# A graph layer on one core: edge attributes and window sums on ScalarE's DMA queue, and other requests moved in time

## The chip, the core and the metric

The kernel runs on one core of a Trainium2 chip. A core has five instruction queues. TensorE (PE) multiplies matrices, VectorE (DVE) and ScalarE (ACT) work on vectors, GpSimd (POOL) here issues gathers, and SyncE (SP) here issues plain DMA transfers. ScalarE can issue plain transfers as well. Each queue works in order and waits on semaphores that the others raise. The metric is the time of the whole program on the device in microseconds (us), the median of several runs.

## The reference

x has 12,500 nodes of 128 features, and there are 400,000 edges, sorted by target. Cut to what matters, in float32:

```
h       = relu(layernorm(x))
msg_src = h @ w_src + b_src;   msg_dst = h @ w_dst
rad     = silu(silu(edge_attr @ w1 + b1) @ w2 + b2) @ w3 + b3      # 400000 x 128 from 32 attributes
m       = (msg_src[src] + msg_dst[dst]) * edge_weight * rad
a, v    = m @ w_a + b_a, m @ w_v + b_v                             # 8 heads of 16 each
score   = sum over a head of smooth_leaky_relu(a) * alpha_dot
att     = softmax of score over the edges of one target
out     = x + segment_sum(v * att, dst) @ w_proj + b_proj
```

## The kernel before

**Node stage.** The nodes go in 25 groups of up to four 128-row blocks (`quads`). x is loaded whole by eight SP transfers (L157, L158). For each group i, `norm` (L231, ACT) makes h, `turn` transposes it (L240 PE, L243 DVE), and `products` multiplies by both weights (L255 PE), copies the result into a tile `ms` (L261 ACT, L259 DVE for some) and asks SP for the two stores to the tables t_src and t_dst (L266). `ms` has four buffers, so a copy waits until the stores from four groups earlier have landed. After group 1 SP issues `load_targets` (L178 to L185, five transfers) and then `load_weights` (L195 to L205). After group 12 stands `fits` (a test of the sorted targets on DVE, a small product on PE, and the load of the sections' first and last targets into `eb`), and after group 20 `cuts`, which reads `eb` and some of the weights.

**Edge stage.** `windows()` goes through 400 pairs; a pair is 1000 edges, two sections of 500. `step(k)` writes one iteration out in the order in which each engine meets its instructions; nothing reorders them later. Its steps are shifted against each other: loads are asked for some pairs ahead, the gathers four and five ahead, the first MLP layers three to one ahead, and the second half, with `c = k - 12`, is twelve pairs behind. In the order of the code, step k has on SP the store of the 128 x 136 sums of pair c-1 into `win` (`store_win`, L926), the store of half of them into `agg` at a row that is read from a table first (`store(c-1, 0)`, L929 and L930), the edge weights of pair k+3 (`load_w`, L717), the rows of targets of pair k+3 (`load_md`: two `value_load` of a row number, L721, and two transfers of 64 x 128, L723), in odd steps the targets of two pairs (`load_d`, L711), the attributes of pair k+6 (`load_e`, L706, 125 x 8 x 32 elements, which lie in runs of 128 bytes), every eighth step a row of marks (`load_sm`, L852), and the second half of the sums (`store(c-1, 1)`). From step 40 on, every eight steps, a block of x is loaded (`load_x`, L937, at the sixth of the eight steps) and two steps later has a bias added on DVE and is stored (`add_x`, L944, L945).

Then comes the arithmetic: `split_md` 0 (L729 ACT: rows of targets of pair k+1 to bf16), `weights` (L888 ACT), `mlp3` (L794 PE, L798 DVE), `sources(k, 1)` (L807 PE: four transposes of gathered rows), `gather(k+4, 1)` (L743 POOL: four gathers into the buffer that `sources(k, 1)` has just released), `message` (L815 PE, L820 DVE into `mT`), `values(c, 0)` (L907 PE, L909 DVE), `split_md` 1 (L732 DVE), `alphas(k, 0)` (L824 PE, L826 ACT into `sl`, L828 DVE), `split_md` 2 (L734 ACT), `mlp1(k+2)` (L762 PE, L765 ACT), `values(c, 1)`, `one_hot(c)` (L894, L897 DVE), `sources(k+1, 0)`, `gather(k+5, 0)`, `alphas(k, 1)`, `mlp2(k+1)` (L777 PE, L780 ACT), `one_hot_T` (L787 DVE), `split_md` 3 (L736 DVE), `sums(c)` (L918 PE, L922 ACT into `ob`, three buffers), `e_T(k+3)` (L753 PE, L755 ACT: the transposed attributes), and in odd steps `scores` (L835 PE, L838 ACT, and the store L840 by SP). `mlp1`, `mlp2` and `mlp3` use the same PSUM tile, so the product of each waits until ACT or DVE has read the one before.

**Lanes.** All plain transfers share eight semaphores in turn. A transfer waits for the one before it on its semaphore, besides the tiles that it needs. A transfer on ACT's queue waits in the same way, and what follows it on that queue waits with it.

**Last stage.** After pair 399 fourteen more steps empty the second half, while the sums of sections that share a target are put together from `win` (`rows_load`, L1074) and scattered into `agg`; then `fin` reads `agg`, multiplies by w_proj and stores the output.

Of the kernel before, what the change touches and what calls it, by code (L numbers as in the profile page):

```python
# [21 lines left out]
F32 = mybir.dt.float32  # L22
# [8 lines left out]
P = 128  # L31
C = 128
# [24 lines left out]
def gnn_kernel(ctx: ExitStack, tc: tile.TileContext, a: dict, out: bass.AP):  # L57
    nc = tc.nc
# [19 lines left out]
    win = dram.tile([NS * W, ROW], F32, name="win")  # L78
# [18 lines left out]
    Q = len(quads)  # L97
# [51 lines left out]
    with tc.tile_pool(name="node", bufs=2) as np_, tc.tile_pool(name="node1", bufs=1) as n1, \  # L149
# [26 lines left out]
        def load_targets():  # L176

            nc.sync.dma_start(out=cur[:, 1:CC + 1], in_=dst.rearrange("(p c) -> p c", p=P))  # L178
            at = dst[CC - 1:CC]
            with nc.allow_non_contiguous_dma(reason="single targets"):  # L180
                nc.sync.dma_start(out=cur[1:P, 0:1], in_=bass.AP(at.tensor, at.offset, [[CC, P - 1], [1, 1]]))
                for f in range(2):
                    nc.sync.dma_start(out=base[:, f, :], in_=dst_h[f:f + 1, :, 0])
                at = dst[0:1]
                nc.sync.dma_start(out=ends, in_=bass.AP(  # L185
                    at.tensor, at.offset, [[8 * SEC, 100], [SEC, 8], [SEC - 1, 2]]))

        def load_weights():
            for name, t in wt.items():
                ap = a[name]  # L190
                if name == "b_src":
                    ap = ap.rearrange("o c -> c o")
                elif name == "b_proj":
                    ap = ap.to_broadcast([P, C])
                nc.sync.dma_start(out=t, in_=ap)  # L195
            for f in range(2):
                for q in range(2):
                    o = (2 * q + f) * RAD
                    nc.sync.dma_start(out=w1b[o:o + RAD, f * FC:(f + 1) * FC], in_=a["fc_w1"])
                s = slice(f * FC, (f + 1) * FC)  # L200
                for q in range(2):
                    nc.sync.dma_start(out=w2b[s, q * FC:(q + 1) * FC], in_=a["fc_w2"])
                nc.sync.dma_start(out=w3b[s, :], in_=a["fc_w3"])
                nc.sync.dma_start(out=b12[s, 0:1], in_=a["fc_b1"])
                nc.sync.dma_start(out=b12[s, 1:2], in_=a["fc_b2"])  # L205
# [40 lines left out]
        def products(i):  # L246
            t0, t1 = quads[i]
            hT = hTs.pop(i)
            ms = np_.tile([P, 2, 4, C], F32, name="ms", bufs=4)
            for v0 in range(t0, t1, 2):  # L250
                vs = range(v0, min(v0 + 2, t1))
                pm = nps.tile([P, 2, 2, C], F32, name="pm", bufs=4)
                for t in vs:
                    n = rows(t)
                    nc.tensor.matmul(pm[:n, t - v0], hT[:, t - t0, :n], w_nodes, start=True, stop=True)  # L255
                for n, u0, u1 in blocks(v0, vs[-1] + 1):
                    o, q = ms[:n, :, u0 - t0:u1 - t0, :].rearrange("p k j c -> p j k c"), pm[:n, u0 - v0:u1 - v0]
                    if v0 % 16 == 2:
                        nc.vector.tensor_copy(o, q)  # L259
                    else:  # L260
                        nc.scalar.copy(o, q)  # L261
            f1 = min(t1, NF)
            for k, table in enumerate((t_src, t_dst)):
                tv = table[0:NF * P, :].rearrange("(p t) c -> p t c", t=NF)
                if t0 < f1:
                    nc.sync.dma_start(out=tv[:, t0:f1, :], in_=ms[:, k, 0:f1 - t0, :])  # L266
                if t1 > NF:
                    nc.sync.dma_start(out=table[NF * P:N, :], in_=ms[:tail, k, NF - t0, :])
# [63 lines left out]
        for i in range(Q):  # L332
            if i % 2 == 0 and 4 * i + G < NB:
                stats(4 * i + G, min(4 * i + 2 * G, NB))
            if i + 2 < Q:
                norm(i + 2)
            if i + 1 < Q:
                turn(i + 1)
            products(i)
            if i == 1:  # L340
                load_targets()
                load_weights()
            if i == 12:
                fits()
            if i == 20:
                cuts()
# [313 lines left out]
    def windows():  # L660
        src_t = src.rearrange("(t p) -> t p", p=T)
        dst_t = dst.rearrange("(t p) -> t p", p=T)
        ea_t = ea.rearrange("(k j p) c -> k p j c", j=8, p=T)
        dst_p = dst.rearrange("(k f e) -> f k e", f=2, e=SEC)
        ew_p = ew.rearrange("(k e) o -> o k e", e=PR)
        with tc.tile_pool(name="wk2", bufs=2) as sp, tc.tile_pool(name="ps", bufs=1, space=PSUM) as pp, \
                tc.manual_schedule(), ExitStack() as held:
            lp = held.enter_context(tc.tile_pool(name="ld", bufs=2))
            prep, e_g, d_g, w_g, md, gath = {}, {}, {}, {}, {}, {}
            eTs, h1s, h2s, ohT, m3, mr, mTs, als, S_all, sms, Ps, Pem, pvx, ohs, accs, xs, Ms, pms = (  # L670
                {} for _ in range(18))
# [31 lines left out]

            def load_e(k):
                e_g[k] = lp.tile([T, 8, RAD], F32, name="e_t", bufs=4)
                nc.sync.dma_start(out=e_g[k], in_=ea_t[k])  # L706

            def load_d(g):
                d_g[g] = lp.tile([P, 2, SEC], I32, name="d_b")
# [7 lines left out]
                nc.sync.dma_start(out=w_g[k], in_=ew_p[:, k, :].to_broadcast([P, PR]))  # L717

            def load_md(k):
                md[k] = lp.tile([P, C], F32, name="md", bufs=4)  # L720
                at = [nc.sync.value_load(base[0:1, f, k:k + 1]) for f in range(2)]  # L721
                for f in range(2):
                    nc.sync.dma_start(out=md[k][f * W:(f + 1) * W, :], in_=t_dst[ds(at[f], W), :])  # L723
# [199 lines left out]
                accs[c] = ob  # L923

            def store_win(c):
                nc.sync.dma_start(out=win[c * P:(c + 1) * P, :], in_=accs[c])  # L926

            def store(c, f):
                at = nc.sync.value_load(base[0:1, f, c:c + 1])  # L929
# [17 lines left out]
            def has(k):  # L947
                return 0 <= k < NP
# [5 lines left out]
            def step(k):  # L954
                c = k - LAG
                if has(c - 1):
                    store_win(c - 1)
                    store(c - 1, 0)

                if k % 16 == 4 and has(k + 12):  # L960
                    prep_load((k + 12) // 16)
                if has(k + 3):
                    load_w(k + 3)
                    load_md(k + 3)
                if k % 2 and has(k + 3):
                    load_d((k + 3) // 2)
                if has(k + 6) and k >= -4:
                    load_e(k + 6)
                if has(k + 4) and (k + 4) % MP == 0:
                    load_sm((k + 4) // MP)  # L970
                if has(c - 1):
                    store(c - 1, 1)
                if 0 <= 2 * k < NZ:
                    for i in range(2 * k, min(2 * k + 2, NZ)):
                        zero(i)
                if k % 16 == 8 and has(k + 8):
                    prep_make((k + 8) // 16)
                i, q = divmod(k - 40, MP)
                if 0 <= i < Q and q == 5:
                    load_x(i)  # L980
                if 0 <= i < Q and q == 7:
                    add_x(i)
                if has(k + 1):
                    split_md(k + 1, 0)
                if has(c):
                    weights(c)
                rad = mlp3(k) if has(k) else None
                if has(k):
                    sources(k, 1)
                if has(k + 4):  # L990
                    gather(k + 4, 1)
                if has(k):
                    message(k, rad)
                if has(c):
                    values(c, 0)
                if has(k + 1):
                    split_md(k + 1, 1)
                if has(k):
                    alphas(k, 0)
                if has(k + 1):  # L1000
                    split_md(k + 1, 2)
                if has(k + 2):
                    mlp1(k + 2)
                if has(c):
                    values(c, 1)
                    one_hot(c)

                if has(k + 1):
                    sources(k + 1, 0)
                if has(k + 5):  # L1010
                    gather(k + 5, 0)
                if has(k):
                    alphas(k, 1)
                if has(k + 1):
                    mlp2(k + 1)
                    one_hot_T(k + 1)
                    split_md(k + 1, 3)
                if has(c):
                    sums(c)
                m, r = divmod(k, MP)  # L1020
                if has(k - MP):
                    if r == 1:
                        softmax_up(m - 1)
                    elif r == 2:
                        softmax_down(m - 1)
                        softmax_exp(m - 1)
                    elif r == 3:
                        softmax_T(m - 1)
                if has(k + 3):
                    e_T(k + 3)  # L1030
                if has(k) and k % 2 == 1:
                    scores(k)
# [300 lines left out]
```

## Time and profile before

| | |
|---|---|
| median of 9 runs | 5890.25 us (5867.07 to 5921.33) |
| profiled execution | 5903.68 us, its span 5901.9 us |
| PE busy | 4619.1 us (78%) |
| POOL busy, 3200 gathers and little else | 3114.7 us (53%) |
| DVE busy | 3096.8 us (52%) |
| ACT busy | 1907.3 us (32%) |
| transfers on SP's queue | 572.15 MB in 796,664 packets |
| mean granted TensorE clock | 0.890 |

A row of a group names line, engine, operation, what is written and read, and how often; then its busy time, the mean of one in ns, and the idle time of the engine just before it with what ended that. "DVE rad <- PE p" in the list of waits means that DVE was idle before `rad` until PE finished `p`. In a timeline the first number is the start in us and the second the duration; what stands in brackets is the engine's idle time before. Issuing a transfer does not count as busy time. The profiled execution took 13.4 us more than the median of the runs, which is within their spread.

### The profile page before, as it was taken

The numbers are of one execution on the slowest core, as the hardware profiler recorded it, in microseconds if no ns is written. First come the engines' busy times: TensorE is split into PE (matmuls) and PEld (weight loads), VectorE is DVE, ScalarE is ACT, GpSimd is POOL, SyncE is SP. The second block draws the span as 40 slices with busy tenths as digits, with TensorE's granted clock in tenths as the row PEclk, the third lists the DMA queues.
The fourth block names the chain that finished last, engine by engine and source line by source line (L and its number), as shares of the span: only waits on it lengthen the run. The fifth ranks groups of instructions, "written<-read, shape, count | busy, mean of one in ns | idle before, by whom it ended". The sixth has DMA issues, their size and how long they took to land.

```text
span 5901.9 us, 88079 instructions
## 1 busy us (share of the span) xinstructions
PE 4619.1 (78%) x29692; PEld 2535.9 (43%) x29692; DVE 3096.8 (52%) x6005; ACT 1907.3 (32%) x4595; POOL 3114.7 (53%) x3223
## 2 busy tenths in 40 slices
PE   5588787787888788777877787888877878878774
PEld 3244444444444444444444444444444444444444
DVE  5355555555555555554555554555555555555556
ACT  4233333333333333333333333333333333333321
POOL 1655555555555555555555555555555555555510
PEclk8789989899898999888898998988898989998887
DMA  5565555555555555555555555555555555555533
GB/s 183 152 150 133 132 136 141 130 132 136 138 136 135 140 132 141 141 127 130 139 129 134 139 133 124 135 134 131 132 129 127 135 129 134 137 134 131 129 85 144
DMA packets 901338, 794.77 MB, mean 135 GB/s; under 512 B 530270, under 2 KB 776974, under 8 KB 900746
## 3 DMA queue, kind: packets, MB, share of 16 engines
q1 hardware_dynamic: 796664, 572.15, 36.1%
q0 software_dynamic: 102816, 210.37, 17.3%
q10 hardware_dynamic: 1394, 6.53, 0.3%
q8 instruction: 234, 3.83, 0.3%
q14 instruction: 230, 1.88, 0.1%
HBM read 648.39 MB, written 140.67 MB: 134 GB/s over the span
## 4 chain that ended last, share of the span: by engine, by line
PE 71%; another core or an unknown queue 8%; DVE 8%; issue 7%; ACT 3%; DMA 2%; SPq 1%; POOL 0%; ACTq 0%; POOLq 0%; DVEq 0%
PE V L907 15%; PE pa L824 13%; PE p L794 8%; PE pm L807 8%; PE misc L918 7%; PE pm L815 5%; PE misc L835 4%; PE p L762 4%; PE p L777 4%; PE m L753 2%; DVE mT L820 2%; DVE rad L798 1%; DVE pvx L909 1%; ACT sl L826 1%
## 5 line engine op out<-in xcount | busy, mean ns | idle before, releaser
L743 POOL DMA_INDIRECT gs<-t_src,idx x3200 | 3100.3, 969 | 2553.1 <-PE pm L807 1158.1
L826 ACT ACTIVATE sl<-pa,c_b_a 128x500 f32<-128x500 f32 x800 | 541.9, 677 | 2403.1 <-PE pa L824 1267.0
L824 PE MATMUL pa<-mT,c_w_a 128*128 128x500 f32 x1600 | 917.8, 658 | 419.8 <-DVE mT L820 297.3
L798 DVE SCALAR_TENSOR_TENSOR rad<-p,c_fc_b,w_b 128x500 f32<-128x500 f32 x800 | 553.2, 733 | 1152.7 <-PE p L794 707.0
L907 PE MATMUL V<-c_w_v,mT 128*125 128x128 f32 x6208 | 980.7, 306 | 182.8 <-DVE pvx L909 161.6
L907 PEld LDWEIGHTS V<-c_w_v,mT 128*125 128x125 f32 x6208 | 823.1, 206 | 502.1 <-issue 273.5
L828 DVE SCALAR_TENSOR_TENSOR al<-pa,sl 128x500 f32<-128x500 f32 x800 | 542.1, 678 | 633.9 <-ACT sl L826 364.3
L909 DVE TENSOR_TENSOR pvx<-V,Pem 125x512 f32<-125x512 f32 x776 | 532.8, 687 | 590.3 <-remote 165.6
L820 DVE SCALAR_TENSOR_TENSOR mT<-pm,c_b_src,rad 128x500 f32<-128x500 f32 x800 | 554.6, 732 | 181.6 <-remote 60.8
L918 PE MATMUL misc<-pvx,oh 125*64 125x136 f32 x6400 | 476.0, 292 | 147.7 <-DVE oh L897 80.3
L807 PE MATMUL pm<-ident,gs 125*128 125x125 f32 x3200 | 560.4, 303 | 1.5 <-DMA gs<-t_src,idx 1.5
L807 PEld LDWEIGHTS pm<-ident,gs 125*128 125x128 f32 x3200 | 404.0, 156 | 351.2 <-issue 348.2
L794 PE MATMUL p<-h,w3b 64*128 64x500 f32 x1600 | 505.5, 712 | 41.7 <-ACT h L780 38.8
L918 PEld LDWEIGHTS misc<-pvx,oh 125*64 125x64 f32 x6400 | 372.1, 141 | 314.8 <-issue 202.6
L824 PEld LDWEIGHTS pa<-mT,c_w_a 128*128 128x128 f32 x1600 | 263.3, 207 | 478.7 <-DVE mT L820 334.0
L835 PE MATMUL misc<-al,w_s 128*32 128x500 f32 x1600 | 255.5, 707 | 258.8 <-ACT ob L922 159.6
L815 PE MATMUL pm<-ohT,m 64*128 64x500 bf16 x2400 | 341.7, 393 | 0.0
L780 ACT ACTIVATE h<-p,b 128x500 f32<-128x500 f32 x400 | 269.8, 674 | 137.4 <-remote 120.7
L922 ACT COPY ob<-misc 128x136 f32<-128x136 f32 x400 | 109.0, 272 | 634.9 <-PE m L753 315.9
L762 PE MATMUL p<-eT,w1b 64*128 64x250 f32 x1600 | 309.9, 468 | 1.0 <-ACT eT L755 0.5
L777 PE MATMUL p<-h,w2b 64*64 64x250 f32 x3200 | 276.1, 417 | 9.3 <-ACT h L765 8.0
L765 ACT ACTIVATE h<-p,b 128x500 f32<-128x500 f32 x400 | 272.9, 682 | 31.4 <-remote 10.9
(145 smaller groups left out, 3268.7 us busy)
## 6 DMA issues: line engine op xcount, KB each, us to landing
w_b<-in_edge_weight SPq DMA_DIRECT2D x400, 500.0 KB
d_b<-in_dst SPq DMA_DIRECT2D x400, 250.0 KB
gs<-t_src,idx POOLq DMA_INDIRECT x3200
e_t<-in_edge_attr SPq DMA_DIRECT2D x400, 125.0 KB
sc_d<-Sp SPq DMA_DIRECT2D x200, 250.0 KB
win<-ob SPq DMA_DIRECT2D x400, 68.0 KB
agg<-ob SPq DMA_DIRECT2D x800, 33.5 KB
md<-t_dst SPq DMA_DIRECT2D x800, 32.0 KB
```

The source lines that it names most:

```text
L743: nc.gpsimd.indirect_dma_start(out=gs[:, j, :], out_offset=None, in_=t_src[:, :], in_offset=bass.IndirectOffsetOnAxis(ap=idx[:, t:t + 1], ...
L762: nc.tensor.matmul(p1[:, q, 0:2 * T], w1b[s, :], eTs[k][s, :], start=True, stop=True)
L794: nc.tensor.matmul(p3[:, f, 0:SEC], w3b[s, :], h2s[k][s, :], start=True, stop=True)
L798: nc.vector.scalar_tensor_tensor(rad[:, s], p3[:, f, 0:SEC], b3, w_g[k][:, s], op0=ALU.add, op1=ALU.mult)
L807: nc.tensor.matmul(pms[k, f][:, t * T:(t + 1) * T], gs[:T, t, :], ident[:T, :T], start=(t == 0), stop=False, is_transpose=True, skip_group ...
L815: nc.tensor.matmul(pm[f], m3[k][s, j, :], ohT[k][s, :], start=False, stop=(j == 2), skip_group_check=True)
L820: nc.vector.scalar_tensor_tensor(mTs[k][:, s], pm[f], b_n, rad[:, s], op0=ALU.add, op1=ALU.mult)
L824: nc.tensor.matmul(pa, w_a, mTs[k][:, f * SEC:(f + 1) * SEC], start=True, stop=True)
L826: nc.scalar.activation(sl, pa, AF.Silu, bias=b_a, scale=1.0)
L907: nc.tensor.matmul(V[:, t, :], mTs[c][:, o:o + T], w_v, start=True, stop=True)
L909: nc.vector.tensor_mul(pvx[c][:, f, :, 0:C].rearrange("p t (h k) -> p t h k", h=H), V.rearrange("p t (h k) -> p t h k", h=H), Pem[c // MP] ...
L918: nc.tensor.matmul(acc[f * W:(f + 1) * W, :], ohs[c][:, f * TS + t, :], pvx[c][:, f, t, :], start=(t == 0), stop=(t == TS - 1), skip_group ...
```

## The change

`ms` gets six buffers instead of four. `load_targets` comes after group 5 and `load_weights` after group 9, instead of both after group 1; `fits` comes after group 15 instead of 12. In the edge stage `load_e` and `store_win` are issued by ACT instead of SP, and stand between `alphas(k, 0)` and `split_md` 2, that is between L826 and L734 on ACT's queue. The two first attribute loads ahead of the loop go to ACT as well. `load_md` asks for pair k+4 instead of k+3 and has five buffers instead of four. `load_x` comes at the first of the eight steps instead of the sixth, seven steps ahead of `add_x`. The transfers are the same in number and size.

```diff
--- before.py
+++ after.py
@@ -246,7 +246,7 @@
         def products(i):
             t0, t1 = quads[i]
             hT = hTs.pop(i)
-            ms = np_.tile([P, 2, 4, C], F32, name="ms", bufs=4)
+            ms = np_.tile([P, 2, 4, C], F32, name="ms", bufs=6)
             for v0 in range(t0, t1, 2):
                 vs = range(v0, min(v0 + 2, t1))
                 pm = nps.tile([P, 2, 2, C], F32, name="pm", bufs=4)
@@ -337,10 +337,11 @@
             if i + 1 < Q:
                 turn(i + 1)
             products(i)
-            if i == 1:
+            if i == 5:
                 load_targets()
+            if i == 9:
                 load_weights()
-            if i == 12:
+            if i == 15:
                 fits()
             if i == 20:
                 cuts()
@@ -703,7 +704,7 @@
 
             def load_e(k):
                 e_g[k] = lp.tile([T, 8, RAD], F32, name="e_t", bufs=4)
-                nc.sync.dma_start(out=e_g[k], in_=ea_t[k])
+                nc.scalar.dma_start(out=e_g[k], in_=ea_t[k])
 
             def load_d(g):
                 d_g[g] = lp.tile([P, 2, SEC], I32, name="d_b")
@@ -717,7 +718,7 @@
                 nc.sync.dma_start(out=w_g[k], in_=ew_p[:, k, :].to_broadcast([P, PR]))
 
             def load_md(k):
-                md[k] = lp.tile([P, C], F32, name="md", bufs=4)
+                md[k] = lp.tile([P, C], F32, name="md", bufs=5)
                 at = [nc.sync.value_load(base[0:1, f, k:k + 1]) for f in range(2)]
                 for f in range(2):
                     nc.sync.dma_start(out=md[k][f * W:(f + 1) * W, :], in_=t_dst[ds(at[f], W), :])
@@ -923,7 +924,7 @@
                 accs[c] = ob
 
             def store_win(c):
-                nc.sync.dma_start(out=win[c * P:(c + 1) * P, :], in_=accs[c])
+                nc.scalar.dma_start(out=win[c * P:(c + 1) * P, :], in_=accs[c])
 
             def store(c, f):
                 at = nc.sync.value_load(base[0:1, f, c:c + 1])
@@ -954,18 +955,16 @@
             def step(k):
                 c = k - LAG
                 if has(c - 1):
-                    store_win(c - 1)
                     store(c - 1, 0)
 
                 if k % 16 == 4 and has(k + 12):
                     prep_load((k + 12) // 16)
                 if has(k + 3):
                     load_w(k + 3)
-                    load_md(k + 3)
+                if has(k + 4):
+                    load_md(k + 4)
                 if k % 2 and has(k + 3):
                     load_d((k + 3) // 2)
-                if has(k + 6) and k >= -4:
-                    load_e(k + 6)
                 if has(k + 4) and (k + 4) % MP == 0:
                     load_sm((k + 4) // MP)
                 if has(c - 1):
@@ -976,7 +975,7 @@
                 if k % 16 == 8 and has(k + 8):
                     prep_make((k + 8) // 16)
                 i, q = divmod(k - 40, MP)
-                if 0 <= i < Q and q == 5:
+                if 0 <= i < Q and q == 0:
                     load_x(i)
                 if 0 <= i < Q and q == 7:
                     add_x(i)
@@ -997,6 +996,10 @@
                     split_md(k + 1, 1)
                 if has(k):
                     alphas(k, 0)
+                if has(k + 6) and k >= -4:
+                    load_e(k + 6)
+                if has(c - 1):
+                    store_win(c - 1)
                 if has(k + 1):
                     split_md(k + 1, 2)
                 if has(k + 2):
```

## The prediction

> **What bounds the kernel now.** I read first the page's engine line and chain, then the waits, then timelines of three places: the node stage, the middle, and the end of the gathers.
>
> ```profile
> span 5901.9 us, 88079 instructions
> PE 4619.1 (78%) x29692; PEld 2535.9 (43%) x29692; DVE 3096.8 (52%) x6005; ACT 1907.3 (32%) x4595; POOL 3114.7 (53%) x3223
> PE 71%; another core or an unknown queue 8%; DVE 8%; issue 7%; ACT 3%; DMA 2%; SPq 1%; POOL 0%; ACTq 0%; POOLq 0%; DVEq 0%
> ```
>
> PE carries the chain; SP, whose queue the change lightens, carries 1% (59 us). The list of waits says why:
>
> ```profile
> SPq L840 <- ACT m L729: 859.7, 156, 10.9
> ACT ob L922 <- DMA agg<-ob: 14.2, 2, 7.1
> ACT m L729 <- DMA md<-t_dst: 4.5, 1, 4.5
> ```
>
> SP stands idle 859.7 us before L840, waiting for ACT's scores, while engines waited for the rows of targets once, for 4.5 us, and for a store of sums for 14.2 us. In the pairs that still have loads and gathers, a step takes (5695.3 - 138.6)/399 = 13.9 us by the first and last L780. PE alone needs less, as the steps after the last gather show, and the middle shows what is lost:
>
> ```profile
> 5668.00 1.11 PE L794 MATMUL p<-h,w3b 64*128 64x500 f32 x4
> 5677.28 1.11 PE L794 MATMUL p<-h,w3b 64*128 64x500 f32 x4
> ...
> 3010.00:3015.00 5.00, 0.71 (x7) 0.52 (x5) 1.35 (x3) 0.00 (x0) 3.78 (x5) 1.00 0.71 191
> 3015.00:3020.00 5.00, 4.68 (x18) 2.66 (x19) 2.61 (x6) 1.55 (x3) 0.81 (x1) 0.66 0.76 158
> ```
>
> Without gathers a step is 9.28 us. From 3010 to 3015 PE, DVE and ACT stand still together while POOL works (the columns after the length are PE, PEld, DVE, ACT, POOL, granted clock, DMA share, GB/s), and in the next five the granted clock is 0.66. POOL's timeline there shows eight gathers in a row, 3005.92 to 15.80, 1.25 us from start to start. Counting breaks of over 1.6 us between starts, from 300 to 5600 us, I find 521 runs of four gathers and 80 of eight; 65 of the eights, and hardly any four, hold a gap of over 3.9 us in PE's completion signals. A run of eight comes when a step's second four are released before its first are done, that is, when PE is quick. The middle is thus PE's work, plus a penalty that POOL's gathers impose. Why they do it the trace doesn't say.
>
> **The change part by part.** The sum is against 5903.7, the profiled execution (its span and 1.8 around it).
>
> *Head.* The two loads fill SP's queue after group 1:
>
> ```profile
> 20.43 0.45 SPq L178 DMA_DIRECT2D cur<-in_dst  x1
> ...
> 28.76 1.33 SPq L195 DMA_DIRECT2D c_b_src<-in_b_src  x1
> ...
> 46.80 0.51 SPq L266 DMA_DIRECT2D t_src<-ms  x1
> ...
> 50.04 1.07 ACT L261 COPY ms<-pm 128x512 f32<-128x512 f32 x2 [13.04 <-DMA t_dst<-ms]
> ```
>
> `load_targets` takes 8.3 us, `load_weights` 18.0, so the stores of group 2 go out at 46.8 and ACT waits 13.04 us for a buffer. Elsewhere ACT paces the stage at 6.8 us for two groups (the rstd rows at 14.17, 20.91, 27.71, 34.52), 3.4 each. After the change group 9 issues its stores at about 17.1 + 9 x 3.4 = 47.7 and the weights hold SP until 65.7. Six buffers carry groups 10 to 15; group 16 wants the buffer of group 10 at 71.5, and that store, issued at 65.7, lands by 68.5 (50.04 less 47.36 is 2.7 for such a one). So that wait goes. `load_targets` at 34 finds x landed, so the 5.83 in its L183 goes too, under buffers. Next late is `fits`, whose DVE work (3.41 and 3.41) still stops ACT for 7.8, at group 15 as at 12. Its `eb` load, at about 81, has until `cuts`, near 92; the same load before was issued at 79.0 and read at 110.97. I take -13.0, with ends -13 and -8 (eb or the catching-up of stores late by one store's 5 us).
>
> *Start of the edge stage.* SP loses three attribute loads (4.2 us from 124.22), so targets come earlier; ACT issues two of them after its last copy (120.8). POOL starts its first 40 gathers when their indices are made (127.42) and runs without a break to 177.3, and ACT stands from 144.9 to 176.8. All this only moves with the head: 0. Ends: -5 (the 4.51 before L729) and +3, if two issues fall on ACT before its 176.81.
>
> *ACT in the steps.* 400 attribute loads and 400 stores. Rows of SP price them, and those of ACT the place:
>
> ```profile
> 3004.30 0.46 SPq L706 DMA_DIRECT2D e_t<-in_edge_attr  x1
> ...
> 3025.31 0.43 SPq L926 DMA_DIRECT2D win<-ob  x1
> ...
> 3002.34 0.68 ACT L826 ACTIVATE sl<-pa,c_b_a 128x500 f32<-128x500 f32 x1 [3.13 <-PE V L907]
> 3002.92 0.29 ACT L734 CAST m<-mr 128x128 bf16<-128x128 f32 x1
> 3003.11 0.69 ACT L765 ACTIVATE h<-p,b 128x500 f32<-128x500 f32 x1
> ```
>
> With gaps of 0.04 the pair takes 0.97 us. Behind it stand L734 and L765 and, later, the second `sl`. DVE wants L734's result at L736, 3.5 us later even in the tightest hundredth of the steps. PE needs L765 before L777, as they share a PSUM tile: from the end of L765 to L777 is 1.41 us in the median; to the next `sl`, 1.9. Summed over the 382 steps that I could pair, a delay of 0.5 us costs what exceeds this slack, 2.9 us; 1.0 costs 7.9; 1.3, 15; 1.7, 99; 2.5, 337. Waits of a queue run ahead of its engine (DVE's wait for its L820 is recorded at 3010.28, inside a `rad` from 3010.15 to 3010.89), so I expect the issues to begin under `sl`, which leaves 0.97 - 0.5 = 0.5 us: +3, with ends 0 and +99 (both issues at the slowest row of L706, 0.90). Their lane waits are, in the built order, almost all for transfers of the step before: the second `agg` store, itself late by 12 us at most of a step's start, lands before ACT gets there. The attributes are used three steps later and `ob` has three buffers, so neither a later nor an earlier issue is felt.
>
> *SP in the steps.* 400 x 0.97 = 388 us of SP's time go. They enlarge the 859.7 us in which it waits anyway: 0. Lower end -50: the chain's 59 us on SP less the 26 that are head, and the 14 of ACT for stores.
>
> [...]
>
> *Rows of targets and x.* The earlier request for rows can remove the 4.5 us in the start, counted there. DVE's idle time before L944 is 0.0 over 26 times, so x is never late; its issue (0.35) moves to another step of the same queue: 0 for both.
>
> *Tail.* In the emptying steps SP itself is late: from 5709.65 to 5740.06 it issues five stores to `win` (0.58, 0.36, 0.55, 0.54, 0.36) between the `agg` stores that the chain runs through: -2.4, ends -4 and 0.
>
> *Sum.* -13.0 + 0 + 3 + 0 - 2.4 = -12.4: 5891.3 for the execution, 5890.25 - 12.4 = 5878 for the median. About 0.3% (17.7 us) is what a measurement tells from no change.
>
> **The rivals.**
> A, the sum: 5862 to 5895, from its ends without the far ones.
> B, fewer penalties: SP issues fewer instructions while POOL runs, or ACT's delay keeps two runs of four apart. For: the penalty depends on some microseconds of spacing. Against: neither POOL's nor PE's queue changes its order. [...]
> C, the other side: ACT's issue becomes the wait before L777. It decides from 1.41 us of delay; at 1.7 the price is 99, less 15: 5974; at 2.5 it would be 6212. For: in the stalls SP's own issues take 0.69 to 0.84 (141.51, 159.13), and two at that price reach 1.7. Against: ACT issues after the stall, not in it.
> D, the head gives nothing since the store queue stalls later: within A, 5890.
>
> [...]
>
> **How the numbers follow.** A 0.42, of which 0.15 lies under 5872.6; B 0.31, all faster; C 0.25, all slower; D 0.02. Faster 0.46, same 0.28 (0.27 of A and D's 0.02, rounded), slower 0.26 with 0.01 for A's far end. The range 5770 to 5975 leaves out the far ends of B and C, about 0.2; A's own is 5862 to 5895.
>
> **What would show it.** Right: the 13.04 before L261 gone and POOL's first gather near 114; L765 about 0.5 us later after `sl`, L777 unmoved; SP's wait before L840 over 1000 us; 70 to 90 runs of eight; a mean step of 13.9. Wrong: a mean step off by over 0.1 us (40 us in all), whichever way, or PE waiting at L777 for ACT's L765.

## The result

The changed kernel takes 6200.49 us (median of 10 runs, 6179.91 to 6248.9) where the kernel before takes 5902.56 (31 runs). The ratio is 1.053, with a 95% interval of 1.0499 to 1.056: 298 us slower, where the prediction had 12 us faster and a range that ended at 5975. Ratios, here and below, leave out slow runs (over some 1.5% above the fastest of the same kernel), and are not the quotients of the medians beside them. The profiled execution has a span of 6223.3 us, against 5901.9 before.

Its page shows first that the work did not grow:

```profile
span 6223.3 us, 87450 instructions
PE 4699.4 (76%) x29692; PEld 2558.6 (41%) x29692; DVE 3097.2 (50%) x6005; ACT 1932.6 (31%) x4595; POOL 3111.7 (50%) x3223
```

DVE and POOL are busy as long as before, ACT for 25 us more and PE for 80. Of the 321.4 us of span, some 241 are idle time of PE. By the first and last L795, a step takes 14.756 us on the mean where it took 13.927; 399 steps at 0.829 are 331 us, so the whole loss lies in the steps. From here on lines are those of the changed kernel, which lie one further down: L765 is now L766, L777 is L778.

The list of waits of the changed kernel (engine and what it was to do, what ended the wait, then us in total, times and the longest) has three entries that were not there, or were small:

```profile
ACT m L735 <- issue: 911.0, 303, 8.7
PEld p L778 <- ACT h L766: 755.4, 285, 9.7
PE p L778 <- ACT h L766: 508.5, 275, 8.1
```

In the kernel before, the entries for the same two instructions were:

```profile
ACT m L734 <- DVE mr L732: 6.5, 31, 0.4
PE p L777 <- ACT h L765: 8.0, 3, 5.1
```

The list of SP's queue of the changed kernel has this one:

```profile
SPq L841 <- ACT m L730: 1971.0, 184, 14.4
```

ACT stands 911 us before L735, the instruction that follows the two new issues, and for nothing that the profile can name: "issue". PE waits at L778 for ACT's L766, which stands behind L735. SP's idle time before its store of scores has more than doubled, from 859.7. The timeline shows what ACT does in those 911 us:

```profile
3010.46 0.68 ACT L827 ACTIVATE sl<-pa,c_b_a 128x500 f32<-128x500 f32 x1 [4.46 <-PE pa L825]
3010.46 0.27 ACTq L707 DMA_DIRECT2D e_t<-in_edge_attr  x1
3010.83 2.83 ACTq L927 DMA_DIRECT2D win<-ob  x1
3013.69 0.30 ACT L735 CAST m<-mr 128x128 bf16<-128x128 f32 x1 [2.56 <-issue]
3013.90 0.67 ACT L766 ACTIVATE h<-p,b 128x500 f32<-128x500 f32 x1
...
3014.62 0.65 PE L778 MATMUL p<-h,w2b 64*64 64x250 f32 x8 [1.24 <-ACT h L766]
```

Issuing the attributes takes 0.27 us. Issuing the 128 rows of `win` right behind takes 2.83. L735 and L766 come after it, and PE, which had ended its L825, stands 1.24 us for L766. One step earlier the same row reads 5.14 us, and PE stood 3.61. Over the whole run, by the view of that one line (count, then shortest, median and longest in ns):

```profile
L927 ACTq DMA_DIRECT2D win<-ob x400: 326/3032/9647, 345.2 to 6120.4; - x134
```

From 300 to 5600 us its mean is 3.35 us. The same transfer was issued by SP in 0.46 us on the mean in the kernel before. What differs is the transfer ahead of it on its queue. The attributes of a pair lie in 1000 runs of 128 bytes. In the records of the transfers, L927's issue ends in the median when 562 of these 1000 have begun to move (quarters of the steps: 512 and 644), 3.46 us after the issue of the attributes. I call this the hold. It is not a wait for a semaphore: of the 381 L927 that took over 1 us, only 1 ended within 0.6 us after a change of a semaphore that it waits for.

The trace of the kernel before had the hold too, on SP, in the very stretch from which the prediction took its prices (SP's timeline from 3000 to 3030 us). The first of these rows stands directly behind the attributes of 3004.30, which the prediction showed:

```profile
3004.81 2.14 SPq L852 DMA_DIRECT2D sm<-same  x1
...
3014.05 0.51 SPq L706 DMA_DIRECT2D e_t<-in_edge_attr  x1
3015.90 2.63 SPq L930 DMA_DIRECT2D agg<-ob  x1
```

What SP issued behind the attributes took 2 us or more on the mean: L852, every eighth step, 2.0 on the mean of 48, and L930 otherwise, 2.39 on the mean of 331. The median of all 800 L930 is 0.35. SP had idle time to pay for it (859.7 us before L840 alone), and so nothing looked wrong.

### The profile page after: what moved, and what is told of

Same layout as the page of the kernel before. It is cut to its first block, busy times and chain, and to the rows that moved or that the text cites. A ratio compares the mean times of both kernels' runs of the same rounds, so it can differ in the third digit from the quotient of the medians.

```text
span 6223.3 us, 87450 instructions
## 1 busy us (share of the span) xinstructions
PE 4699.4 (76%) x29692; PEld 2558.6 (41%) x29692; DVE 3097.2 (50%) x6005; ACT 1932.6 (31%) x4595; POOL 3111.7 (50%) x3223
## 5 line engine op out<-in xcount | busy, mean ns | idle before, releaser
L825 PE MATMUL pa<-mT,c_w_a 128*128 128x500 f32 x1600 | 895.4, 643 | 350.3 <-DVE mT L821 222.7
L908 PE MATMUL V<-c_w_v,mT 128*125 128x128 f32 x6208 | 936.6, 297 | 96.7 <-DVE pvx L910 83.8
L908 PEld LDWEIGHTS V<-c_w_v,mT 128*125 128x125 f32 x6208 | 783.5, 198 | 401.5 <-issue 243.7
L778 PE MATMUL p<-h,w2b 64*64 64x250 f32 x3200 | 290.5, 437 | 621.9 <-ACT h L766 508.5
L919 PE MATMUL misc<-pvx,oh 125*64 125x136 f32 x6400 | 552.8, 324 | 66.6 <-DVE oh L898 48.4
L795 PE MATMUL p<-h,w3b 64*128 64x500 f32 x1600 | 535.4, 751 | 24.2 <-ACT h L781 16.7
L808 PE MATMUL pm<-ident,gs 125*128 125x125 f32 x3200 | 542.9, 296 | 4.3 <-issue 2.5
L919 PEld LDWEIGHTS misc<-pvx,oh 125*64 125x64 f32 x6400 | 430.1, 157 | 240.6 <-issue 205.3
L778 PEld LDWEIGHTS p<-h,w2b 64*64 64x64 f32 x3200 | 89.1, 142 | 970.4 <-ACT h L766 755.4
L735 ACT CAST m<-mr 128x128 bf16<-128x128 f32 x400 | 118.9, 297 | 1145.9 <-issue 911.0
L825 PEld LDWEIGHTS pa<-mT,c_w_a 128*128 128x128 f32 x1600 | 257.2, 202 | 400.2 <-DVE mT L821 252.4
L781 ACT ACTIVATE h<-p,b 128x500 f32<-128x500 f32 x400 | 271.6, 679 | 153.6 <-issue 48.0
```

What stands on the lines that cost most here:

```text
L778: nc.tensor.matmul(p2[o, h, 0:2 * T], w2b[s, o], h1[s, f * 2 * T:(f + 1) * 2 * T], start=True, stop=True)
L795: nc.tensor.matmul(p3[:, f, 0:SEC], w3b[s, :], h2s[k][s, :], start=True, stop=True)
L808: nc.tensor.matmul(pms[k, f][:, t * T:(t + 1) * T], gs[:T, t, :], ident[:T, :T], start=(t == 0), stop=False, is_transpose=True, skip_group ...
L825: nc.tensor.matmul(pa, w_a, mTs[k][:, f * SEC:(f + 1) * SEC], start=True, stop=True)
L908: nc.tensor.matmul(V[:, t, :], mTs[c][:, o:o + T], w_v, start=True, stop=True)
L919: nc.tensor.matmul(acc[f * W:(f + 1) * W, :], ohs[c][:, f * TS + t, :], pvx[c][:, f, t, :], start=(t == 0), stop=(t == TS - 1), skip_group ...
```

## The experiments

Three theories stood against each other. HELD: the issue behind the attributes is held until their runs have drained to some number, and ACT is held with it. PLACE: two issues at this place are too much for ACT, held or not. OTHER: the loss comes from the head, the rows of targets or x. In the code `...` stands for lines that are not shown, and an old place of a moved line is not always shown.

The chips that the runs fell on are not alike. The kernel before takes 5882.98 us on one (called A here) and 5904.7 on another (B), and 4684.8 and 4658.25 in two groups on a third (C). On which chip the result above was measured is not on record; its 5902.56 us are like those of A and B. So each run is compared with the kernel before on its own chip and in its own group.

### Chip C: the order, the parts and the size of the runs

**The swapped order.** `win` first, the attributes behind it, both on ACT.

```
                     alphas(k, 0)
+                if has(c - 1):
+                    store_win(c - 1)
                 if has(k + 6) and k >= -4:
                     load_e(k + 6)
-                if has(c - 1):
-                    store_win(c - 1)
                 if has(k + 1):
                     split_md(k + 1, 2)
```

> Theories, all runs of this group. HELD: on ACT's queue the issue of `win` stands right behind that of the attributes and is held for a mean of 3.35 us, until over half of the 1000 runs of 128 bytes have begun to move; L735 and L766 stand behind it, and PE waits for L766 at L778. PLACE: any two issues between the first `sl` and L735 are too much, held or not. OTHER: the loss comes from the head, the rows of targets or x, not from ACT's queue. Here the changed kernel has `store_win` ahead of `load_e`, both still on ACT. HELD: each issue takes 0.3 to 0.6 us, what follows the attributes on the queue comes a step later, the time is 5870 to 5915. PLACE and OTHER: still about 6200.

Measured: 4520.48 against 4684.8 us, 0.9658 (0.9635 to 0.9682).

**Nothing on ACT.** Both back on SP, at their old places.

```
+                    store_win(c - 1)
                     store(c - 1, 0)
...
+                if has(k + 6) and k >= -4:
+                    load_e(k + 6)
                 if has(k + 4) and (k + 4) % MP == 0:
                     load_sm((k + 4) // MP)
```

> The changed kernel with `load_e` and `store_win` back on SP at their old places; head, rows of targets and x as changed. HELD and PLACE: 5870 to 5905; by the prediction's terms for the head (-13.0) and 0 for the rest it is 0.998 of the kernel before. OTHER: about 6200.

Measured: 4664.52 us, 0.9957 (0.9944 to 0.997).

**Only `win` back on SP.**

```
             def store_win(c):
-                nc.scalar.dma_start(out=win[c * P:(c + 1) * P, :], in_=accs[c])
+                nc.sync.dma_start(out=win[c * P:(c + 1) * P, :], in_=accs[c])
```

> The changed kernel with only `store_win` back on SP at its old place; the attributes are still asked for by ACT. HELD: one issue of 0.27 us per step on ACT with no transfer behind it for a step, 5870 to 5915. PLACE: half of the loss, about 6040. OTHER: about 6200.

Measured: 4486.72 us, 0.9574 (0.9555 to 0.9593).

**Runs of 512 bytes.** Each partition now takes four consecutive edges of a section instead of four that lie 125 apart, so that their attributes are one run of 512 bytes; the second layer's result is written with a stride, which puts the edges in order again.

```
-        ea_t = ea.rearrange("(k j p) c -> k p j c", j=8, p=T)
+        ea_t = ea.rearrange("(k f p t) c -> k p f (t c)", f=2, p=T, t=TS)
...
-                nc.scalar.activation(h2s[k].rearrange("x (q h p) -> x h q p", q=2, h=2),
+                nc.scalar.activation(h2s[k].rearrange("x (p q h) -> x h q p", q=2, h=2),
```

> The changed kernel with the attributes of a pair laid out in 250 runs of 512 bytes where there were 1000 of 128, the same bytes; the second layer's result is written with a stride so that the edges keep their order. HELD, if the hold goes by the number of runs (the next issue came free in the traces with about 440 runs not yet begun): L927 falls to 0.3 to 0.6 us, and the time to 5870 to 5930, the strided write of L781 included. HELD, if it goes by bytes: L927 stays near 3 us and the time near 6200. PLACE and OTHER: about 6200.

Measured: 4460.0 us, 0.9522 (0.9504 to 0.954), with the order of the changed kernel, `win` right behind the attributes. The issue of `win`:

```profile
L927 ACTq DMA_DIRECT2D win<-ob x400: 326/400/906, 292.7 to 4362.1; - x134
```

The absolute times of all four missed, since they had been written for the other kind of chip. What the ratios say at once is that PLACE is false on this chip (with two issues at that place the swapped order and the long runs are faster than with none on ACT), and OTHER too. But the changed kernel had not yet been run on this chip, so it might have been no slower there.

**The changed kernel on chip C**, in a later group.

> The changed kernel once more. HELD: 1.05 to 1.06 on a chip where the kernel before takes 5900; 1.03 to 1.10 where it takes 4685 (4520 for the swapped order, and 300 to 640 for the hold).

Measured: 5602.78 against 4658.25 us, 1.203 (1.1991 to 1.207). HELD had the sign and the order, but the price was far over what I had allowed for: 1082 us above the swapped order (of the earlier group), not 300 to 640, and a ratio of 1.203, not 1.03 to 1.10. The page's span and busy times and PE's largest wait, first of the changed kernel on chip C and then of the swapped order on the same chip:

```profile
span 5590.6 us, 87450 instructions
PE 4509.0 (81%) x29692; PEld 2480.9 (44%) x29692; DVE 3084.2 (55%) x6005; ACT 1949.1 (35%) x4595; POOL 3166.0 (57%) x3223
```

```profile
PE p L778 <- ACT h L766: 819.2, 384, 19.6
```

```profile
span 4517.0 us, 87471 instructions
PE 4164.7 (92%) x29692; PEld 2323.5 (51%) x29692; DVE 3079.6 (68%) x6005; ACT 1965.8 (44%) x4595; POOL 3106.2 (69%) x3223
```

```profile
PE p L778 <- ACT h L766: 85.4, 75, 17.3
```

PE's wait at L778 grew by 734 us. Span less busy time, PE's idle time, is 1081.6 against 352.3, a growth of 729: hardly any of the wait was made up elsewhere. The other 344 us of the 1074 are PE's busy time for the same instructions. The granted clock was 0.902 on the mean against 0.976. So the changed kernel loses twice here: PE stands 729 us longer, and is busy 344 us longer with the same instructions.

### Chip A: the kernel before takes about as long as in the result

> The kernel before takes about 5900 us on one chip and about 4685 on another, so the changed kernel itself is run beside its variants. HELD: slower than the kernel before on both kinds of chip; where that one takes 5900, 1.053 again; where it takes 4685, the order with `win` first took 4520, and a hold of 3.1 us beyond `sl` in each step against the 1.41 from L766 to L778 adds 300 to 640: 4820 to 5160. PLACE and OTHER have fallen where the kernel before takes 4685; they would say 4520, that is, that the changed kernel is slower only on the other chip.

Measured: 6244.31 against 5882.98 us, 1.0608 (1.0559 to 1.0657).

> The changed kernel with `store_win` ahead of `load_e`, both on ACT. HELD: the loss is gone on either kind of chip: 5870 to 5915 where the kernel before takes 5900, 4520 where it takes 4685. If the loss of the slow chip has another cause that the fast chip doesn't show: about 6200 there.

Measured: 5878.61 us, 0.9967 (0.9935 to 0.9999). The same two issues, in the swapped order, on ACT's timeline:

```profile
3027.40 0.68 ACT L827 ACTIVATE sl<-pa,c_b_a 128x500 f32<-128x500 f32 x1 [4.44 <-PE pa L825]
3027.41 0.36 ACTq L927 DMA_DIRECT2D win<-ob  x1
3027.80 0.42 ACTq L707 DMA_DIRECT2D e_t<-in_edge_attr  x1
3028.26 0.30 ACT L735 CAST m<-mr 128x128 bf16<-128x128 f32 x1 [0.18 <-issue]
3028.47 0.67 ACT L766 ACTIVATE h<-p,b 128x500 f32<-128x500 f32 x1
```

Both issues nearly fit under `sl`: ACT stands 0.18 us before L735 instead of 2.56. Nothing was removed: the same instructions, one line moved, 366 us by the medians.

> The changed kernel with the attributes in 250 runs of 512 bytes, in the order of the changed kernel (attributes first, `win` behind them). HELD by the number of runs: as the swapped order, 5830 to 5915 where the kernel before takes 5900, 4460 where it takes 4685. HELD by bytes: like the changed kernel itself in the same group.

Measured: 5837.01 us, 0.991 (0.9875 to 0.9946). The issue of `win` takes 401 ns in the median, where it takes 3050 in the changed kernel on this chip. The runs are what counts, not the bytes, on this chip as well (their number and their length change together here).

**The kernel before with long runs, all on SP.**

> The kernel before with nothing changed but the attributes in 250 runs of 512 bytes, all on SP. If SP is held behind its own attribute load in the same way (L930's second store and L852 take 2.4 and 2.0 us there) and this costs time, the kernel gets faster: 4500 to 4600 where the kernel before takes 4685, and 5750 to 5900 where it takes 5900. If SP's hold is hidden, as the prediction had it, it stays within 0.5% of the kernel before.

Measured: 5873.37 us, 0.998 (0.9957 to 1.0004). The two lines that stood behind the attributes on SP, in the kernel before and then with long runs:

```profile
L930 SPq DMA_DIRECT2D agg<-ob x800: 3/353/6987, 346.9 to 5797.6; - x160
...
L852 SPq DMA_DIRECT2D sm<-same x50: 1322/1900/3085, 128.6 to 5562.7; - x50
```

```profile
L930 SPq DMA_DIRECT2D agg<-ob x800: 3/338/750, 348.0 to 5738.5; - x160
...
L852 SPq DMA_DIRECT2D sm<-same x50: 3/602/1230, 127.9 to 5503.6; - x50
```

The longest L930 falls from 6987 to 750 ns, and the median L852 from 1900 to 602. From 300 to 5600 us L930's issues add up to 209 us where they took 906. These 700 us of SP's time bought nothing that can be measured on chip A: SP's hold was hidden there, and ACT's was not.

### A dose between, and a best version (chip C)

**Runs of 256 bytes**, 500 of them, in the changed kernel's order.

```
+        ea_t = ea.rearrange("(k f q p h) c -> k p f q (h c)", f=2, q=2, p=T, h=2)
...
+                nc.scalar.activation(h2s[k].rearrange("x (q p h) -> x h q p", q=2, h=2),
```

> The changed kernel with the attributes in 500 runs of 256 bytes, in its own order on ACT. With 1000 runs the next issue came free when about 560 had begun, 440 not; with 250 runs it took its usual 0.4 us. If a fixed number of about 440 may be outstanding, 60 have to begin first, some 1.9 us after the issue (the first begins after 1.5 to 1.8 us): L927 takes a mean of 1.0 to 1.7 us, which the 1.41 us of slack before L778 nearly covers: 0.99 to 1.01 of the kernel before on a chip where that takes 5900, 0.955 to 0.975 where it takes 4685. If the hold lasts for a fixed share of the runs: L927 2.0 to 2.5 us, 1.01 to 1.03 on the first kind of chip.

Measured: 4468.2 us, 0.9597 (0.9577 to 0.9616). L927 takes 0.61 us on the mean, less than either reading had: the next issue comes free in the median before a single one of the 500 has begun. With 1000 it had come free with about 440 not begun, with 250 it takes 0.4 us. A fixed share of the runs is out as what ends the hold, and so is a fixed number of 440 not yet begun, which was my estimate from the 1000 runs. What ends it was not shown.

**Attributes on ACT in long runs, `win` on SP.**

> Both findings together: the attributes on ACT in 250 runs of 512 bytes, `win` on SP as before, head, rows of targets and x as changed. HELD: nothing on ACT's queue is held, 0.985 to 0.995 of the kernel before on a chip where that takes 5900, 0.945 to 0.955 where it takes 4685.

Measured: 4455.01 us, 0.9569 (0.9549 to 0.9589). In microseconds it is the lowest on chip C; by the ratio to the kernel before of its own group the long runs with both issues on ACT (0.9522) are ahead, and short runs with `win` on SP (0.9574) are as good as it. The long runs with both issues on ACT are also faster than the kernel before on chip A.

### What is left when ACT's part is taken out

> The changed kernel with `load_e` and `store_win` on SP at their old places: head, rows of targets and x alone. Prediction's terms: -13.0 to -15, 0.9975 of the kernel before on a chip where that takes 5900; 0.9957 was measured where it takes 4685.

Measured on chip C: 4645.47 us, 0.9976 (0.996 to 0.9993).

> Head, rows of targets and x alone, for the chip on which the kernel before takes 5900: prediction's terms -13.0 to -15, 0.9975. Where it takes 4685, 0.9957 and 0.9976 were measured.

Measured on chip B: 5902.25 us, 0.9971 (0.9927 to 1.0015). The expected 0.9975 lies in both intervals; the first group on chip C had 0.9957, whose interval ends at 0.997. So head, rows and x cost nothing: what makes the changed kernel slower is ACT's part.

### The same hold, at another place

The issues go behind `weights`, where ACT is idle (4.46 us before the first `sl` in the changed kernel's rows above); the attributes are still ahead of `win`.

```
                 if has(c):
                     weights(c)
+                if has(k + 6) and k >= -4:
+                    load_e(k + 6)
+                if has(c - 1):
+                    store_win(c - 1)
```

> The changed kernel with both issues, the attributes first and `win` behind them, moved on ACT's queue from behind the first `sl` to behind `weights` (L889), ahead of the first `sl`. ACT is idle there: in a step at full pace L889 ends 1.3 us after the step's first L795 and the first `sl` starts at 4.4. The hold stays (L927 3 to 3.6 us). If what a hold costs is only what stands behind it beyond its slack: 4.1 us of issue against 3.1 of slack, 1.0 to 1.5 us in half of the steps: 1.00 to 1.03 of the kernel before on the slow chip, 0.98 to 1.08 on the fast one, far below the changed kernel's 1.06 and 1.20. If a held ACT costs the same wherever it stands: 1.06 and 1.20.

Measured on chip B: 5967.4 against 5904.7 us, 1.0128 (1.0072 to 1.0183). PE's wait for L766 is 1.0 us in all. So with idle time behind it the hold no longer reaches PE by that path. But the hold was shorter here too (L927 2.40 us on the mean, not 3.35), and the run doesn't say how much of the gain is due to the place. Against the swapped order (0.9967, on chip A) the 400 holds cost 0.0161 of 5904.7, 95 us; the changed kernel lost 366 us on chip A. By the prediction's table a delay shorter by the same 0.95 us would have cost less at the old place too: counted in the same way, it gives 198 us at 2.05 and 503 at 3.0, and 366 times 198/503 is 144, an estimate. The place would then account for about 50 us and the shorter hold for the rest. Why the hold was shorter was not looked into.

## Why the prediction was wrong

**The step that failed** is "ACT in the steps", +3 with ends 0 and +99. Its place, its path and its method were right: it named L734 and L765 as what stands behind, the shared PSUM tile as the reason, 1.41 us as the slack, and a table of losses by delay. The price was wrong: the term measured 366 us on chip A (the changed kernel against the swapped order), where +3 was expected. "With gaps of 0.04 the pair takes 0.97 us" came from one row of each transfer in SP's timeline. The row of `win`, 0.43 at 3025.31, was taken where it stood first in its step, 11 us after the last attributes; the change puts it directly behind them. The rows that showed the price of that position, 2.14 and 2.63, stood in the same timeline between the two that were quoted. The prediction's own text had a sign of it as well: "three attribute loads (4.2 us from 124.22)" are 0.49, 1.80 and 1.83 us, and the two long ones stand directly behind another attribute load. With the measured 0.27 and 3.35, less what lies under `sl`, L766 starts on the mean 3.16 us after the end of the first `sl`, where it started 0.17 after: a delay of 3.0, for which the table, continued, gives 337 at 2.5 and 538 at 3.1. The upper end of the term, +99, took both issues at "the slowest row of L706", which says nothing of the issue behind it, and was not the slowest either (1.80 and 1.83, as just said).

**The measured loss is less than the table** on the slow chips, and why shows in PE's idle time. On chip A, PE's idle time before L778 is 594 us in the changed kernel and 11 in the swapped order, by the gaps in PE's records. PE's whole idle time, span less busy time, grows only from 1279.4 to 1549.5, by 270. So 313 us of the waits at L778 took the place of other waits of PE; 67 more are PE's busy time. On chip C nearly nothing was replaced (729 of 734 us stayed), 344 us more of PE's busy time came on top, and the price rose to 1082 us.

The prediction also put the waits for earlier transfers on ACT's queue at nothing. In the swapped order that held on chip A. On chip C they are small but there: ACT waits before L735 for the landing of `agg` (49.7 us in all) and of `win` (47.2), and PE 85.4 us at L778.

**Rival C** was the right one, with its mechanism (ACT's issue becomes the wait before L777) and its condition, 1.41 us; it even stated 6212 for a delay of 2.5. That this is near the 6200 measured is luck: the delay was 3.0, for which the table gives more, and part of the waits replaced others. It had 0.25, and its argument against, "ACT issues after the stall, not in it", looked for a long issue in the wrong place. The range took its price at 1.7 us, 5974, and left 6212 out.

**Rival B** gave the range its lower end. No run shows the price of a stall that lies under that 5770; what the runs show is fewer long runs of gathers (65 of eight, where there were 80) in a kernel that takes 298 us more, at a mean granted clock of 0.877 where it was 0.890.

**The head** was right. The 13.04 us before L261 are gone, the 7.8 of `fits` moved to group 15 as worked out (7.87 measured, at 76.36), and POOL's first gather comes at 115.45 with nothing on ACT (chip B) and at 117.65 in the changed kernel, for 127.42 before; "near 114" was 1.5 and 3.7 us too early. The first L778 stands 13.0 and 11.0 us earlier (124.3 and 126.3, for 137.4). The 2 us between the two lie in the start of the edge stage, where the prediction had an end of +3.

**SP in the steps**: 0 was right on chip A, by the kernel before with long runs. On chip C it was not. There, with nothing on ACT, the maximum over a section waits for the scores that SP writes and reads back:

```profile
DVE M L857 <- DMA S<-sc_d: 139.7, 42, 12.8
```

With the attributes on ACT and nothing held, this entry is gone, and the swapped order is 144 us faster than that kernel. So moving the two transfers was worth some 3% there. That SP is close to the bound on this chip fits the entry, but isn't shown: the kernel before with long runs on SP was not run on chip C, which would tell SP's hold from the number of its issues.

**Rows of targets, x**: nothing that can be seen. **The tail**, -2.4, did not come: from the last L795 to the end it is 205.7 us before and between 204.6 and 209.5 in the changed kernel, the swapped order and the one with nothing on ACT. SP's five issues were not what set the end there, though the chain ran past them.

**The sum without the failed term** held for the swapped order on chip A: -12.4 of 5890 is 0.998, and it measured 0.9967 (0.9935 to 0.9999). The long runs, with nothing held at all, measured 0.991 (0.9875 to 0.9946) there, some 40 us less than the sum; where these come from is not known. Of the signs to look for, SP's wait before L840 did pass 1000 us (1971), and L765 did come later, by six times what was expected. Runs of eight gathers were 65 and not 70 to 90 (and 14 for the same kernel on chip A). "A mean step off by over 0.1 us, whichever way, or PE waiting at L777" is what was seen.

## What to carry to other kernels

The price of moving a transfer to another queue was here not in its own row but in the row behind it: in the old trace, look at what follows the transfer on its queue, and in the new order at what will follow it. In this kernel the load in 1000 short runs cost least last on its queue (0.9967 of the kernel before, chip A), more ahead of idle time with `win` behind it (1.0128, chip B), and most in front of `win` on an engine whose next instructions PE waited for (1.0608 on chip A, 1.203 on C). Longer runs for the same bytes removed the hold: behind 250 runs of 512 bytes the next issue took 0.40 us in the median on chips A and C, where it took 3.05 and 3.65 behind 1000 runs of 128.

## What the hardware showed that I had not expected

**The hold on ACT did not reach SP.** While ACT was held behind the attributes (from the end of L707 to that of L927, its last 0.5 us left out), SP began 260 of its L931 issues (300 to 5600 us); they took 0.32 us in the median, against 0.31 for the 454 others. So whatever ACT waited for did not hold up these issues of SP.

**Chips differ by a quarter on the same kernel.** The kernel before took 5883 and 5905 us on chips A and B and 4685 and 4658 on C. The instructions are the same; a stretch of 500 us of the swapped order shows the difference, on chip A and then on chip C (length, then the busy times of PE, PEld, DVE, ACT and POOL, the granted clock, the DMA share, GB/s):

```profile
3000.00:3500.00 500.00, 402.60 (x2664) 219.35 (x2667) 267.28 (x510) 171.46 (x407) 287.12 (x295) 0.92 0.58 139
```

```profile
3000.00:3500.00 500.00, 480.87 (x3501) 264.53 (x3498) 347.50 (x663) 226.28 (x532) 370.47 (x385) 1.00 0.77 175
```

On chip C PE is busy 96% of that stretch at full clock. The stall that the prediction found in long runs of gathers is absent there in this order: of the 71 runs of five or more gathers in a row (many of 32 or 64), one holds a gap of over 3.9 us in PE's completion signals; on chip A 53 of 91 do, in runs of five to nine. So with the same code the stall is frequent on one chip and missing on another. (With nothing on ACT some 13 of 120 such runs on chip C hold a gap, and in the changed kernel more, where ACT's hold stops PE anyway.) What makes the chips differ was not found, and no run here was aimed at it.
